# A graph network kernel planned in ticks: which instructions of a tick come first

## The chip, the cores and the metric

The kernel runs on one core of one Trainium2 chip. The metric is the device time of one launch in microseconds (us). The engines of the core are TensorE (PE, with its weight loads as PEld), VectorE (DVE), ScalarE (ACT), GpSimd (POOL) and SyncE (SP, which here only issues transfers). Each runs its own list of instructions in the order in which the kernel gives them, and waits at an instruction until its inputs are there and its output's buffer is free.

## The reference

There are 64 graphs of 256 nodes with 256 features. Two layers follow each other, each with its own residual.

```python
# layer 0: three steps of a gated graph network, one GRU cell for all of them
h = jnp.maximum(_layernorm(x), 0.0)
A = (adj != 0).astype(x.dtype)
for i in range(3):
    m = jnp.einsum('bnd,de->bne', h, weight[i])
    aggr = jnp.einsum('bst,bsd->btd', A, m)
    gi = aggr @ w_ih.T + b_ih          # split in three: i_r, i_z, i_n
    gh = h @ w_hh.T + b_hh             # split in three: h_r, h_z, h_n
    r, z = sigmoid(i_r + h_r), sigmoid(i_z + h_z)
    n = tanh(i_n + r * h_n)
    h = (1.0 - z) * n + z * h
x = x + h
# layer 1: graph attention, four heads of 64
h = jnp.maximum(_layernorm(x), 0.0) @ W.T + b
logits = leaky_relu(l_src[:, :, None, :] + l_dst[:, None, :, :], 0.2)
probs = softmax(where(adj == 1, logits, -9e15), axis=2)
x = x + einsum('bijh,bjhc->bihc', probs, h)
```

## The kernel before

Two graphs make a pair, and there are 32 pairs. What is wide is 512 columns: two graphs (halves 0 and 1) of 256 nodes each. A tile such as `hT` holds the features on the partitions, in two groups of 128 (`c` = 0, 1), and the nodes of both graphs along the columns.

**The GRU step** is the class `Step` (L365), one object for each pair and layer, with its work cut into `tick_0` to `tick_5`. A `block` (L289) is four f32 matmuls of 128 by 256 that add one weight matrix times one half of the columns to a PSUM bank; the profile counts each of them as two instructions. A `part` (L394) is one such matmul. The two graphs share products: instead of weights times half 0 and weights times half 1, the kernel multiplies sums and differences of the halves and of the weights, and puts the results together with VectorE and ScalarE. That is why there are `T1`, `T2`, `T3`, `T4` (sums of state and aggregate, two groups each) and `T2n`, `T3n`, `T4n` (sums of the state for n's term alone). `state_sums` (L381) makes `T1` and the three n sums. In short:

- `tick_0`: the parts `N00` and `NS1` into bank `qa`, ScalarE's copies `qb` and `m5n`, 16 matmuls that sum the neighbours into `pa`, ScalarE's copy to `aggr`, VectorE's `T3` and `T2`.
- `tick_1`: the parts `N01` and `NS2`, VectorE's sum in `qb` (L435), the block `RH` and its copy.
- `tick_2`: the parts `NS3` and `NS4`, VectorE's `hn` (L445), the block `S1`, `T4`.
- `tick_3`: the block `S2`, VectorE's sum into `pe`, the block `RA`, and the tanh that makes gate r for half 0.
- `tick_4`: the part `N11`, ScalarE's `hn`, the block `RZ`, VectorE's sum into `Z`, the block `S4`, and r for half 1.
- `tick_5`: for each half `input_n` (L469), which has VectorE write (r + 1) times hn into the bank `pn` (L472) and then adds the block `NA` to it; between them the block `ZA` for gate z. Then `new_n`: a tanh on ScalarE and a difference on GpSimd (L484).
- `update(0)` and `update(1)`, four VectorE instructions (L498, L499), write the new state over the old.

`back` (L540) transposes the new state for the next step's neighbour sum, or adds it to x after the last one. Then come the second norm, `values`, `score_rows`, `linked`, `barred_in`, `add_rows`, `maxima` (L685, two VectorE instructions for each head), `leaky`, `exps` and `output` for the attention. Score rows and maxima go through DRAM, to be read back on all partitions.

**The plan.** Nothing orders these pieces but one table, `plan`. Each is put at a tick (`at`, L307) and in one of three phases of that tick; the kernel then walks the ticks, and in each tick the phases in the order of their numbers, and in a phase the later pair first. A new pair starts every `APART` = 18 ticks, and a step of six ticks is followed by six that belong to a step of a neighbouring pair. So a repeat of 18 ticks has three steps: layer 0 of a new pair, layer 2 of the pair before it, and layer 1 of the new pair, while an older pair goes through its attention.

```python
READY, STEP, REST = range(3)
...
for tick in sorted(plan):
    for phase in plan[tick]:
        for _, fn in sorted(phase, key=lambda y: y[0]):
            fn()
```

`STEP` holds the six ticks of a GRU step; norms, sums, updates, maxima, leaky and exps are put in `READY`, transposes, values and output in `REST`. Most tiles have one buffer; x has five, adj two. PSUM has five banks for the step (`gate_bank`) and three for everything else (`bank`).

Of the kernel before, what the change touches and what calls it, by code (L numbers as in the profile page):

```python
# [14 lines left out]
ALU = mybir.AluOpType  # L15
AX = mybir.AxisListType

P = 128
# [8 lines left out]
def gated_gnn_then_gat_kernel(  # L27
# [39 lines left out]
    nc = tc.nc  # L67
    B, N, D = x.shape
# [4 lines left out]
    KD = D // P  # L73
# [3 lines left out]
    T = PB * N  # L77
# [31 lines left out]
    out_rows = out.rearrange("b s d -> (b s) d")  # L109


    def load_adj(p, name):
        at = buf("adj", [P, R, N], f"{name}_{p}", I32)
        nc.sync.dma_start(at, adj_rows[ts(p, T), :].rearrange("(r q) t -> q r t", q=P))
        return at

    def load_x(p):
        xt = buf("x", [P, R, D], f"x_{p}")
        nc.sync.dma_start(xt, x_rows[ts(p, T), :].rearrange("(r q) d -> q r d", q=P))
        return xt  # L120
# [69 lines left out]
    w_a = [const.tile([P, KD, 6 * D], F32, name=f"w_a_{l}") for l in range(L)]  # L190
    RH, RZ = range(2)
    N00, N01, N11, NS1, NS2, NS3, NS4 = range(7)
    RA, ZA, NA, S1, S2, S4 = range(6)
# [95 lines left out]
    def block(pt, w, j, src, start=False):  # L289

        for c in range(KD):
            for k in range(KD):
                nc.tensor.matmul(  # L293
                    pt[:, ts(c, N)], w[:, k, j * D + c * P : j * D + (c + 1) * P], src[:, k, :],
                    start=start and c == 0 and k == 0, stop=(c == KD - 1 and k == KD - 1),
                    skip_group_check=True,
                )
# [1 line left out]

    READY, STEP, REST = range(3)
    SUB = 6
    APART = 3 * SUB
    plan = {}
# [1 line left out]
    def at(tick, phase, p, fn):  # L307
        plan.setdefault(tick, ([], [], []))[phase].append((-p, fn))

    def plan_norm(src, name, p, ticks):  # L310

        v = {}

        def stats(r0):
            def fn():
                if not v:
                    v["st"] = small.tile([P, R, 6], F32, tag="st", name=f"st_{name}")
                    v["mv"] = small.tile([P, R, 2], F32, tag="mv", name=f"mv_{name}")
                for r in (r0, r0 + 1):
                    nc.vector.bn_stats(v["st"][:, r, :], src()[:, r, :])  # L320
                    nc.vector.bn_aggr(v["mv"][:, r, :], v["st"][:, r, :])
            return fn

        def deviation():
            rstd = v["rstd"] = small.tile([P, R], F32, tag="rstd", name=f"rstd_{name}")
            nc.vector.tensor_scalar_add(rstd, v["mv"][:, :, 1], EPS)
            nc.gpsimd.tensor_tensor(rstd, rstd, mhalf, ALU.pow)

        def result():
            xn = v["xn"] = buf("xn", [P, R, D], f"xn_{name}")  # L330
            for r in range(R):
                nc.vector.tensor_scalar(  # L332
                    xn[:, r, :], src()[:, r, :], v["mv"][:, r, 0:1], v["rstd"][:, r : r + 1],
                    op0=ALU.subtract, op1=ALU.mult,
                )

        for t, fn in zip(ticks, (stats(0), stats(2), deviation, result)):
            at(t, READY, p, fn)
        return v
# [19 lines left out]
    def by_c(y):  # L359
        return y.rearrange("q (c n) -> q c n", c=KD)  # L360

    def of(y, i):
        return y[:, :, ts(i, N)]

    class Step:  # L365
# [15 lines left out]
        def state_sums(self):  # L381
            h0, h1 = of(self.hT(), 0), of(self.hT(), 1)
            T1 = self.own("T1", [P, KD, N])
            nc.vector.tensor_sub(T1, h1, h0)  # L384
            T3n = self.own("T3n", [P, N])
            nc.vector.tensor_sub(T3n, h1[:, 1, :], h1[:, 0, :])
            T2n = self.own("T2n", [P, N])
            nc.vector.tensor_sub(T2n, h1[:, 1, :], T1[:, 0, :])
            T4n = self.own("T4n", [P, N])
            nc.vector.tensor_sub(T4n, T2n, h0[:, 1, :])  # L390

# [12 lines left out]
        def tick_0(self, hN, edge):  # L406
            h0 = of(self.hT(), 0)
            q_a, q_b = self.bank("qa"), self.bank("qb")
            self.part(q_a[:, :N], N00, h0[:, 0, :], start=True)
            self.part(q_a[:, N:], NS1, self.T1[:, 0, :])  # L410
            nc.scalar.copy(q_b[:, :N], q_a[:, :N])
            nc.scalar.copy(self.own("m5n", [P, N]), q_a[:, N:])
            aggr = self.own("aggr", [P, KD, T])
            for e in range(KD):
                pt = bank(f"pa_{self.n_}_{e}")
                for i in range(PB):
                    for s in range(KN):
                        for half in range(2):
                            nc.tensor.matmul(  # L419
                                pt[:, ts(i, N)], hN[half][:, i * KN + s, ts(e, P)], edge[:, i * KN + s, :],  # L420
                                start=(s == 0 and half == 0), stop=(s == KN - 1 and half == 1),
                            )
                nc.scalar.copy(aggr[:, e, :], pt)  # L423
            T3 = self.own("T3", [P, KD, N])
            nc.vector.tensor_sub(T3, of(aggr, 1), of(self.hT(), 1))  # L425
            nc.vector.tensor_add(self.own("T2", [P, KD, N]), T3, h0)

        def tick_1(self):
            h0 = of(self.hT(), 0)
            q_a, q_b = self.qa, self.qb  # L430
            self.own("hn", [P, KD, T])
            self.part(q_a[:, :N], N01, h0[:, 1, :])
            self.state_n(0, 0, q_a[:, :N])
            self.part(q_b[:, :N], NS2, self.T2n)
            nc.vector.tensor_add(q_b[:, N:], q_b[:, :N], self.m5n)  # L435
            p_c = self.bank("pc")
            block(p_c, w_h, RH, h0, start=True)
            self.bank("p5")
            nc.scalar.copy(self.bank("pd"), p_c)

        def tick_2(self):
            q_b = self.qb
# [17 lines left out]
        def tick_4(self):  # L460
            Z_ = self.own("Z", [P, KD, T])
            self.part(self.qb[:, :N], N11, self.T4n)
            self.state_n(1, 0, self.qb[:, :N])
            block(self.pd, w_h, RZ, self.T3)
            nc.vector.tensor_add(of(Z_, 1), by_c(self.pd), by_c(self.m5))
            block(self.pe, w_a[self.l], S4, of(self.aggr, 1))
            self.tanh_half(1, self.R, by_c(self.pe), 0)

        def input_n(self, i):  # L469

            p_n = self.bank(f"pn{i}")
            nc.vector.scalar_tensor_tensor(  # L472
                by_c(p_n), of(self.R, i), 1.0, of(self.hn, i), op0=ALU.add, op1=ALU.mult
            )
            block(p_n, w_a[self.l], NA, of(self.aggr, i))

        def new_n(self, i):
            n__ = of(self.hn, i)
# [5 lines left out]
            nc.gpsimd.tensor_sub(of(self.R, i), of(self.hT(), i), n__)  # L484

        def tick_5(self):
            self.input_n(0)
            self.tanh_half(1, self.Z, of(self.Z, 1), KD)
            block(self.pd, w_a[self.l], ZA, self.T4)
            self.new_n(0)  # L490
            self.tanh_half(0, self.Z, by_c(self.pd), KD)
            self.input_n(1)
            self.new_n(1)
# [7 lines left out]
    def plan_pair(p):  # L501
        t0 = APART * p
        v = {}

        def ready(t, fn):
            at(t0 + t, READY, p, fn)
# [4 lines left out]
        def rest(t, fn):  # L511
            at(t0 + t, REST, p, fn)


        if p == 0:
            v["x"], v["adj"] = first
        else:
            rest(-14, lambda: v.update(x=load_x(p), adj=load_adj(p, "adj")))

        def to_edge():  # L520
            v["edge"] = buf("edge", [P, R, N], f"edge_{p}", F32R)
            nc.vector.tensor_scalar(v["edge"], v["adj"], 0.0, None, op0=ALU.not_equal)

        xn_a = plan_norm(lambda: v["x"], f"a{p}", p, [t0 - 8, t0 - 7, t0 - 6, t0 - 5])
        ready(-4, to_edge)
        h = plan_relu_T(xn_a, "hT_a", f"a{p}", p, [t0 - 4, t0 - 3])


# [6 lines left out]
            nc.vector.scalar_tensor_tensor(lo, flat(xn_a["xn"]), 0.0, hi, op0=ALU.max, op1=ALU.subtract)  # L535

        ready(-3, first_hi)
        ready(-2, first_lo)

        def back(l, i):  # L540

# [17 lines left out]
        for l in range(L):  # L559
            g = Step(f"{p}_{l}", l, lambda: h["hT"])  # L560
            t = 2 * SUB * l
            ready(t - 1, g.state_sums)
            step(t, lambda g=g: g.tick_0(v["hN"], v["edge"]))
            for k, fn in enumerate((g.tick_1, g.tick_2, g.tick_3, g.tick_4, g.tick_5), 1):
                step(t + k, fn)
            ready(t + SUB, lambda g=g: g.update(0))
            rest(t + SUB, lambda g=g: g.update(1))
            for i in range(PB):
                rest(t + SUB + 1 + i, back(l, i))

# [152 lines left out]
        for u in units:  # L723
            t = 47 if last and u.start == 0 else 51
# [35 lines left out]

        for t, (i, j) in zip((60, 61, 62, 63), ((0, 0), (0, 1), (1, 0), (1, 1))):
            ready(t, exps(i, j))
        for r, t in enumerate((62, 63, 64, 66)):
            rest(t, output(r))
        rest(67, lambda: nc.sync.dma_start(out_rows[ts(p, T), :].rearrange("(r q) d -> q r d", q=P), v["x"]))


    at(SUB, REST, 0, lambda: step_weights(1))
# [38 lines left out]
```

## Time and profile before

| what | value |
|---|---|
| time, median of 2 runs | 3209.2 us (3208.84 to 3209.55) |
| span of the profiled run | 3207.4 us |
| mean granted TensorE clock | 0.932 |
| L472 on VectorE, 128x512, one | 694 ns |
| state sums on VectorE: `T1`, `T3n`, `T2n`, `T4n` | 671, 420, 415, 425 ns |
| L685 on VectorE, one head's maximum | 512 ns |
| new state, L498 and L499, one | 688 and 692 ns |
| tanh on ScalarE, 128x256, one | 471 ns |
| L484 on GpSimd, one | 1279 ns |

The busy share of an engine is an average over the span, and a busy TensorE need not run at its full clock: the page has a row for the granted clock in forty slices.

```profile
PE   6888888888888888888888888888888888888875
DVE  4456655555655555665555565555555555565554
PEclk8999999999999999999999999999999999999995
```

All slices between the first and the last two look alike, so what is true of one repeat of 18 ticks holds for nearly the whole run. A line of groups (line, engine, operation, out<-in, count | busy us, mean ns | idle before us, releaser) tells how long an engine stood still just before these instructions, and which instruction let it go on.

### The profile page before, as it was taken

How to read it: one execution, taken by the hardware profiler on the slowest of the kernel's cores; microseconds unless marked ns; L12 is line 12 of the kernel's file. 1: busy time of each engine (PE TensorE's matmuls, PEld its weight loads, DVE VectorE, ACT ScalarE, POOL GpSimd, SP SyncE). 2: the span in 40 equal slices, each digit the busy share in tenths (PEclk: the TensorE clock that was granted, in tenths of full speed). 3: DMA queues.
4: the chain of work that ended last, by engine and by line, in shares of the span. 5: the costliest groups of instructions: out<-in, count | busy, mean ns of one | idle time of the engine just before them, and what ended most of it. 6: DMA issues, size and time to landing. Idle time of an engine off the chain costs nothing.

```text
span 3207.4 us, 38372 instructions
## 1 busy us (share of the span) xinstructions
PE 2720.1 (85%) x14074; PEld 2366.8 (74%) x14074; DVE 1823.8 (57%) x4497; ACT 1485.2 (46%) x3077; POOL 567.4 (18%) x518
## 2 busy tenths in 40 slices
PE   6888888888888888888888888888888888888875
PEld 4777777777777777777777777777777777777765
DVE  4456655555655555665555565555555555565554
ACT  1345444454444454444454444454444554444543
POOL 0011111111112121212111212111211111211112
PEclk8999999999999999999999999999999999999995
DMA  2013224342223342233332233432233432243334
GB/s 72 9 50 72 57 67 93 86 93 67 58 68 93 86 93 56 61 76 93 86 90 54 59 82 86 93 84 48 67 87 86 93 80 47 66 92 86 80 80 99
DMA packets 120317, 239.87 MB, mean 75 GB/s; under 512 B 9792, under 2 KB 79424, under 8 KB 120128
## 3 DMA queue, kind: packets, MB, share of 16 engines
q0 software_dynamic: 34272, 132.13, 21.4%
q1 hardware_dynamic: 80160, 102.52, 10.5%
q10 hardware_dynamic: 5696, 2.76, 0.3%
q8 instruction: 111, 1.82, 0.2%
q14 instruction: 78, 0.64, 0.1%
HBM read 219.82 MB, written 17.56 MB: 74 GB/s over the span
## 4 chain that ended last, share of the span: by engine, by line
PE 71%; DVE 22%; ACT 3%; issue 2%; DMA 1%; POOL 0%; ACTq 0%; SPq 0%; DVEq 0%; POOLq 0%
PE pd L293 17%; PE pn L293 13%; PE pc L293 7%; PE p L293 6%; PE po L745 6%; PE qb L395 5%; PE pa L419 4%; PE pv L596 4%; PE pe L293 3%; DVE any L685 2%; PE qa L395 2%; DVE pn L472 2%; DVE T L384 2%; PE pback L548 2%; DVE xn_a L332 2%
## 5 line engine op out<-in xcount | busy, mean ns | idle before, releaser
L293 PE MATMUL pn<-aggr,w_a 128*128 128x256 f32 x1536 | 445.9, 441 | 297.9 <-DVE pn L472 297.9
L293 PEld LDWEIGHTS pn<-aggr,w_a 128*128 128x128 f32 x1536 | 326.5, 218 | 378.1 <-DVE pn L472 325.1
L484 POOL TENSOR_TENSOR R<-hT_a,hn 128x512 f32<-128x512 f32 x192 | 245.6, 1279 | 1517.1 <-ACT hn L481 1493.0
L498 DVE SCALAR_TENSOR_TENSOR R<-Z,R 128x512 f32<-128x512 f32 x192 | 132.2, 688 | 503.1 <-ACT Z L402 501.5
L293 PE MATMUL pd<-T,w_a 128*128 128x256 f32 x1536 | 399.5, 407 | 0.0
L481 ACT ACTIVATE hn<-pn,bi 128x256 f32<-128x256 f32 x384 | 161.3, 471 | 493.7 <-PE pn L293 493.7
L293 PEld LDWEIGHTS pd<-T,w_a 128*128 128x128 f32 x1536 | 318.8, 211 | 53.2
L685 DVE CUSTOM_DVE_ANT_0 any<-drow,noedge 128x256 f32<-128x256 f32 x512 | 262.3, 512 | 18.2 <-DMA drow<-score_dram 9.2
L745 PEld LDWEIGHTS po<-val,zz 128*128 128x128 f32 x2048 | 256.7, 201 | 15.1 <-ACT zz L736 11.9
L745 PE MATMUL po<-val,zz 128*128 128x65 f32 x2048 | 256.0, 281 | 11.1 <-ACT zz L736 11.1
L713 ACT ACTIVATE zz<-zz,val 128x256 f32<-128x256 f32 x512 | 230.9, 507 | 7.7 <-DMA zz<-score_dram 7.7
L758 POOL TENSOR_TENSOR x<-x,o 128x256 f32<-128x256 f32 x128 | 101.0, 789 | 671.9 <-DVE o L753 671.9
L293 PE MATMUL p<-T,w_a 128*128 128x256 f32 x768 | 214.2, 430 | 0.0
L398 ACT ACTIVATE hn<-qb,bhn 128x256 f32<-128x256 f32 x192 | 90.8, 473 | 249.6 <-DVE hn L445 208.2
L402 ACT ACTIVATE R<-pc,brz 128x256 f32<-128x256 f32 x192 | 80.6, 471 | 264.6 <-PE pc L293 264.6
L425 DVE TENSOR_TENSOR T<-aggr,hT_a 128x512 f32<-128x512 f32 x96 | 66.5, 693 | 224.4 <-ACT aggr L423 224.4
L293 PEld LDWEIGHTS p<-T,w_a 128*128 128x128 f32 x768 | 167.0, 217 | 28.6
L402 ACT ACTIVATE R<-pe,brz 128x256 f32<-128x256 f32 x192 | 80.6, 471 | 220.4 <-PE pe L293 220.4
L293 PE MATMUL pc<-aggr,w_a 128*128 128x256 f32 x768 | 181.4, 379 | 0.0
L293 PE MATMUL pc<-hT_a,w_h 128*128 128x256 f32 x768 | 181.4, 379 | 0.0
L293 PE MATMUL pd<-T,w_h 128*128 128x256 f32 x768 | 181.4, 379 | 0.0
L293 PE MATMUL pe<-aggr,w_a 128*128 128x256 f32 x768 | 181.4, 379 | 0.0
(147 smaller groups left out, 5381.7 us busy)
## 6 DMA issues: line engine op xcount, KB each, us to landing
zz<-score_dram POOLq DMA_DIRECT2D x64, 1024.0 KB, 12.0
zz<-topT_dram POOLq DMA_DIRECT2D x62, 1024.0 KB, 9.6
adj<-in_adj_dram SPq DMA_DIRECT2D x64, 512.0 KB
drow<-score_dram SPq DMA_DIRECT2D x64, 512.0 KB
x<-in_x_dram SPq DMA_DIRECT2D x32, 512.0 KB
out_dram<-x SPq DMA_DIRECT2D x32, 512.0 KB
score_dram<-score SPq DMA_DIRECT2D x128, 4.0 KB
topT_dram<-topT SPq DMA_DIRECT2D x128, 2.0 KB
```

What stands on the lines that cost most here:

```text
L293: nc.tensor.matmul(pt[:, ts(c, N)], w[:, k, j * D + c * P : j * D + (c + 1) * P], src[:, k, :], start=start and c == 0 and k == 0, stop=(c ...
L395: nc.tensor.matmul(pt, w_n[:, j, :], src, start=start, stop=True, skip_group_check=True)
L402: nc.scalar.activation(of(dst, i)[:, c, :], src[:, c, :], AF.Tanh, bias=brz[:, g0 + c : g0 + c + 1], scale=0.5)
L419: nc.tensor.matmul(pt[:, ts(i, N)], hN[half][:, i * KN + s, ts(e, P)], edge[:, i * KN + s, :], start=(s == 0 and half == 0), stop=(s == KN ...
L481: nc.scalar.activation(n__[:, c, :], p_n[:, c, :], AF.Tanh, bias=bi[:, 2 * KD + c : 2 * KD + c + 1])
L484: nc.gpsimd.tensor_sub(of(self.R, i), of(self.hT(), i), n__)
L498: nc.vector.scalar_tensor_tensor(d_, of(self.Z, i), 1.0, d_, op0=ALU.add, op1=ALU.mult)
L596: nc.tensor.matmul(pt[:, :VW], hb["hT"][:, k, ts(r, P)], w_val[:, k, :], start=(k == 0), stop=(k == KD - 1),)
L685: nc.vector.tensor_tensor_reduce(any_, drow[r // KN][:, h, :], v["noedge"][:, r, :], 1.0, -3.0e38, ALU.add, ALU.max, accum_out=v["top"][:, ...
L713: nc.scalar.activation(zz[:, h, :], zz[:, h, :], AF.Prelu, alpha=ALPHA, bias=v["val"][:, r, S0 + H + h : S0 + H + h + 1],)
L745: nc.tensor.matmul(po[:, ts(h_, VC)], logits[i][:, j, h_, ts(s, P)], v["val"][:, i * KN + j, ts(h_, VC)], start=(j == 0), stop=(j == KN - 1),)
L758: nc.gpsimd.tensor_add(v["x"][:, r, :], v["x"][:, r, :], o)
```

## The change

The phases change places: in each tick the step's own work now comes first. `T3` and `T2` go from the end of tick 0 to the end of tick 1, the part `NS1` and its copy behind the neighbour sum, and the write of (r + 1) times hn is taken out of `input_n` as `first_n`: half 0 goes into tick 4, half 1 to the top of tick 5. The sums of the state are made at tick 3 of the step in between (`t - 3`) for layers 1 and 2, and `T4n` on its own at tick 2. The second update goes from `REST` to `READY`. The first norm, the edges and the loads of x and adj get other ticks, `first_lo` another phase, and the last row of the output comes a tick earlier. The aim is that instructions for which TensorE waits don't stand behind others in the lists of VectorE and ScalarE.

```diff
@@ -299,7 +299,7 @@
-    READY, STEP, REST = range(3)
+    STEP, READY, REST = range(3)
     SUB = 6
     APART = 3 * SUB
     plan = {}
@@ -386,8 +386,9 @@
             nc.vector.tensor_sub(T3n, h1[:, 1, :], h1[:, 0, :])
             T2n = self.own("T2n", [P, N])
             nc.vector.tensor_sub(T2n, h1[:, 1, :], T1[:, 0, :])
-            T4n = self.own("T4n", [P, N])
-            nc.vector.tensor_sub(T4n, T2n, h0[:, 1, :])
+
+        def last_state_sum(self):
+            nc.vector.tensor_sub(self.own("T4n", [P, N]), self.T2n, of(self.hT(), 0)[:, 1, :])
@@ -407,9 +408,7 @@
             h0 = of(self.hT(), 0)
             q_a, q_b = self.bank("qa"), self.bank("qb")
             self.part(q_a[:, :N], N00, h0[:, 0, :], start=True)
-            self.part(q_a[:, N:], NS1, self.T1[:, 0, :])
             nc.scalar.copy(q_b[:, :N], q_a[:, :N])
-            nc.scalar.copy(self.own("m5n", [P, N]), q_a[:, N:])
             aggr = self.own("aggr", [P, KD, T])
             for e in range(KD):
                 pt = bank(f"pa_{self.n_}_{e}")
@@ -421,9 +420,8 @@
                                 start=(s == 0 and half == 0), stop=(s == KN - 1 and half == 1),
                             )
                 nc.scalar.copy(aggr[:, e, :], pt)
-            T3 = self.own("T3", [P, KD, N])
-            nc.vector.tensor_sub(T3, of(aggr, 1), of(self.hT(), 1))
-            nc.vector.tensor_add(self.own("T2", [P, KD, N]), T3, h0)
+            self.part(q_a[:, N:], NS1, self.T1[:, 0, :])
+            nc.scalar.copy(self.own("m5n", [P, N]), q_a[:, N:])
         def tick_1(self):
             h0 = of(self.hT(), 0)
@@ -437,6 +435,9 @@
             block(p_c, w_h, RH, h0, start=True)
             self.bank("p5")
             nc.scalar.copy(self.bank("pd"), p_c)
+            T3 = self.own("T3", [P, KD, N])
+            nc.vector.tensor_sub(T3, of(self.aggr, 1), of(self.hT(), 1))
+            nc.vector.tensor_add(self.own("T2", [P, KD, N]), T3, h0)
         def tick_2(self):
             q_b = self.qb
@@ -461,18 +462,20 @@
             Z_ = self.own("Z", [P, KD, T])
             self.part(self.qb[:, :N], N11, self.T4n)
             self.state_n(1, 0, self.qb[:, :N])
+            self.first_n(0)
             block(self.pd, w_h, RZ, self.T3)
             nc.vector.tensor_add(of(Z_, 1), by_c(self.pd), by_c(self.m5))
             block(self.pe, w_a[self.l], S4, of(self.aggr, 1))
             self.tanh_half(1, self.R, by_c(self.pe), 0)
+        def first_n(self, i):
+
+            nc.vector.scalar_tensor_tensor(
+                by_c(self.bank(f"pn{i}")), of(self.R, i), 1.0, of(self.hn, i), op0=ALU.add, op1=ALU.mult
+            )
+
         def input_n(self, i):
-
-            p_n = self.bank(f"pn{i}")
-            nc.vector.scalar_tensor_tensor(
-                by_c(p_n), of(self.R, i), 1.0, of(self.hn, i), op0=ALU.add, op1=ALU.mult
-            )
-            block(p_n, w_a[self.l], NA, of(self.aggr, i))
+            block(getattr(self, f"pn{i}"), w_a[self.l], NA, of(self.aggr, i))
         def new_n(self, i):
             n__ = of(self.hn, i)
@@ -484,6 +487,7 @@
             nc.gpsimd.tensor_sub(of(self.R, i), of(self.hT(), i), n__)
         def tick_5(self):
+            self.first_n(1)
             self.input_n(0)
             self.tanh_half(1, self.Z, of(self.Z, 1), KD)
             block(self.pd, w_a[self.l], ZA, self.T4)
@@ -515,14 +519,14 @@
         if p == 0:
             v["x"], v["adj"] = first
         else:
-            rest(-14, lambda: v.update(x=load_x(p), adj=load_adj(p, "adj")))
+            rest(-20, lambda: v.update(x=load_x(p), adj=load_adj(p, "adj")))
         def to_edge():
             v["edge"] = buf("edge", [P, R, N], f"edge_{p}", F32R)
             nc.vector.tensor_scalar(v["edge"], v["adj"], 0.0, None, op0=ALU.not_equal)
-        xn_a = plan_norm(lambda: v["x"], f"a{p}", p, [t0 - 8, t0 - 7, t0 - 6, t0 - 5])
-        ready(-4, to_edge)
+        xn_a = plan_norm(lambda: v["x"], f"a{p}", p, [t0 - 14, t0 - 13, t0 - 13, t0 - 7])
+        ready(-1, to_edge)
         h = plan_relu_T(xn_a, "hT_a", f"a{p}", p, [t0 - 4, t0 - 3])
@@ -535,7 +539,7 @@
             nc.vector.scalar_tensor_tensor(lo, flat(xn_a["xn"]), 0.0, hi, op0=ALU.max, op1=ALU.subtract)
         ready(-3, first_hi)
-        ready(-2, first_lo)
+        rest(-3, first_lo)
         def back(l, i):
@@ -559,12 +563,13 @@
         for l in range(L):
             g = Step(f"{p}_{l}", l, lambda: h["hT"])
             t = 2 * SUB * l
-            ready(t - 1, g.state_sums)
+            ready(t - 3 if l else t - 1, g.state_sums)
+            ready(t + 2, g.last_state_sum)
             step(t, lambda g=g: g.tick_0(v["hN"], v["edge"]))
             for k, fn in enumerate((g.tick_1, g.tick_2, g.tick_3, g.tick_4, g.tick_5), 1):
                 step(t + k, fn)
             ready(t + SUB, lambda g=g: g.update(0))
-            rest(t + SUB, lambda g=g: g.update(1))
+            ready(t + SUB, lambda g=g: g.update(1))
             for i in range(PB):
                 rest(t + SUB + 1 + i, back(l, i))
@@ -760,9 +765,9 @@
         for t, (i, j) in zip((60, 61, 62, 63), ((0, 0), (0, 1), (1, 0), (1, 1))):
             ready(t, exps(i, j))
-        for r, t in enumerate((62, 63, 64, 66)):
+        for r, t in enumerate((62, 63, 64, 65)):
             rest(t, output(r))
-        rest(67, lambda: nc.sync.dma_start(out_rows[ts(p, T), :].rearrange("(r q) d -> q r d", q=P), v["x"]))
+        rest(66, lambda: nc.sync.dma_start(out_rows[ts(p, T), :].rearrange("(r q) d -> q r d", q=P), v["x"]))
     at(SUB, REST, 0, lambda: step_weights(1))
```

## What the change is expected to do

> **What bounds the kernel now.** I read the page's engine shares first, then the waits, then one repeat of the work as stretches, and last the timeline and the chain of waits at one gap.
>
> ```profile
> PE 2720.1 (85%) x14074; PEld 2366.8 (74%) x14074; DVE 1823.8 (57%) x4497; ACT 1485.2 (46%) x3077; POOL 567.4 (18%) x518
> ...
> L293 PE MATMUL pn<-aggr,w_a 128*128 128x256 f32 x1536 | 445.9, 441 | 297.9 <-DVE pn L472 297.9
> L293 PE MATMUL pd<-T,w_a 128*128 128x256 f32 x1536 | 399.5, 407 | 0.0
> L293 PE MATMUL pe<-aggr,w_a 128*128 128x256 f32 x768 | 181.4, 379 | 0.0
> ```
> ```profile
> PE pn L293 <- DVE pn L472: 297.9, 95, 5.4
> PE qb L395 <- DVE qb L435: 117.9, 65, 4.7
> PE ptopT L610 <- DVE top L697: 12.4, 3, 6.1
> ```
>
> TensorE is the busiest engine, and it stands still for 487 us of the span. Two waits are 416 us of that, both on VectorE, which is itself busy only 57%: so VectorE is not too slow, it does other things first. The pn matmuls also run longer than the same matmuls elsewhere (mean 441 ns against 379 for pe).
>
> ```profile
> 1512.50:1547.00 34.50, 29.14 (x145) 25.00 (x143) 23.81 (x58) 16.96 (x39) 5.70 (x6) 0.90 0.05 16
> 1547.00:1579.00 32.00, 30.60 (x168) 26.96 (x167) 15.18 (x30) 19.80 (x39) 8.48 (x7) 1.00 0.68 154
> 1579.00:1611.00 32.00, 25.39 (x132) 22.12 (x131) 17.27 (x52) 9.81 (x20) 3.54 (x4) 0.89 0.31 61
> ```
>
> These stretches (length, then busy PE, PEld, DVE, ACT, POOL, then clock, DMA share, GB/s) are about one repeat of 18 ticks. Where PE has few gaps the clock is 1.00; in the two with gaps it is 0.90 and 0.89. One gap in full, from the timeline and the chain:
>
> ```profile
> 1597.47 0.18 DVE L751 RECIPROCAL rden<-po 128x4 f32<-128x4 f32 x1 [2.56 <-PE po L745]
> 1597.76 0.42 DVE L753 TENSOR_TENSOR o<-po,rden 128x256 f32<-128x256 f32 x1
> 1598.10 0.42 DVE L320 BATCH_NORM_STATS2 st_a<-x 128x6 f32<-128x256 f32 x1
> ...
> 1599.18 0.66 DVE L384 TENSOR_TENSOR T<-hT_a 128x512 f32<-128x512 f32 x1
> ...
> 1600.89 0.42 DVE L685 CUSTOM_DVE_ANT_0 any<-drow,noedge 128x256 f32<-128x256 f32 x1
> ```
> ```profile
> 1595.70 1.75 PE po L745 x16
> 1599.27 0.57 DVE T L384
> 1601.78 0.62 DVE pn L472
> 1602.45 3.78 PE pn L293 x8
> 1606.23 2.75 PE pd L293 x8
> 1608.98 1.73 PE pn L293 x8
> ```
>
> PE ends po at 1597.45 and waits 5 us for one VectorE instruction (L472), which stands behind a norm, the state's sums and the maxima, none of which it needs. Then it pays again: eight pn and eight pd matmuls take 6.53 us where two warm blocks take 3.46.
>
> [...] clock 0.89 to 0.90 where gaps of 3.3 and 5.0 us lie, 1.00 where the longest is 1.4 us, and blocks of 3.78 us beside 1.73. [...] so I count PE by starts of warm blocks, from the chain, and not by its 85%.
>
> **PE's own work in a repeat.** Three layer steps make a repeat: slot A (ticks 0 to 5, a new pair's layer 0), B (layer 2 of the pair before), C (layer 1). From the warm rows of the chain: a block 1.73, two parts 0.86, the 16 aggr matmuls 1.92, po 1.73, two value rows 1.81, a transpose group 0.44. A step is 9 x 1.73 + 7 x 0.43 + 1.92 = 20.5. The rest of a pair is 4 po, 2 x 1.81, ten transpose groups and about 1 us of small ones: 16. So 3 x 20.5 + 16 = 77.4 us. The trace has qa of slot A at 202.13 (pair 2) and 2996.69 (pair 31): 29 repeats of 96.4. So 19.0 us in each are waits and half clock (13 of them the two waits, 416 us over 32).
>
> **The change part by part.** No arithmetic comes or goes; each edit moves instructions.
>
> 1. L472 for the first half goes to tick 4, behind its hn only, ahead of the Z sum; the second half to the top of tick 5. The norms', sums' and maxima's work then comes after them. In B: RA ends at 14.0 us from the slot's start, po at 15.8, N11 at 16.2; ScalarE's hn follows at 16.9 (0.47), VectorE's pn0 at 17.65 (0.69). PE needs it after RZ, S4 and po, 21.4: no wait. pn1 comes after rden and o (0.6) of that po, at 22.9; PE needs it at 24.8. In A pn0 is done about 1.9 us early. In C ScalarE has R, hNhi_a, leaky and hT_a ahead of hn (0.84 + 1.07 + 0.91 + 0.60 from RA's end at 12.9), so hn ends at 16.8, pn0 at 17.5, and PE was ready at 17.2: about 0.45 us stays. The gaps of 1.4, 5.0 and 3.3 us become 0, 0, 0.45.
>
> 2. L435, ahead of the next qb matmul, loses T3 and T2 (1.4 us) in front of it and, being first in tick 1, the maxima (0.8) and in C xn_a (1.7, now a tick earlier). Both updates (4 x 0.69) now come before it in tick 0; the second waits for n's tanh and 1.3 us of GpSimd, and is done 3.4 to 3.8 us into the slot. Behind that wait stand maxima and L435. L435 runs at about 4.7 in B and C, 5.1 in A; PE wants its bank at 5.8 (B, C) and 8.4 (A). No wait, with about 1 us to spare. Its other consumer, ScalarE's hn (L398, 118.8 us behind the update), starts earlier too.
>
> 3. Moving three state sums to tick 3 of A and B puts 1.4 us ahead of the score copy in A, which PE's transpose needs: PE waits about 0.8 us there. This is the one new PE wait I find. In B they lie beside po. T4n (0.42) lies beside the S1 block. For layer 0 sums, edge and noedge (2.9) follow pn1 in C, beside ZA and pn1's block.
>
> 4. NS1 after aggr, tanh ahead of leaky and exps, output one tick earlier: order alone. The ScalarE copies for aggr fit: n's tanh ends 1.0 us into a slot, qb's copy at 2.5 in A's wake (a barred write of 1.06 between), and PE needs it at 3.2.
>
> 5. x and adj load at -20. The adj buffer is free only when edge of the pair before has run, now three ticks later; so the load waits on SyncE for that, with the topT rows queued behind it, and GpSimd's add waits for those. That is some 2 us late, against about three ticks (13 us) until the add. adj has a repeat to land.
>
> Sum: 77.4 + 0.8 + 0.45 = 78.7. I allow 1.0 for small waits that I have not seen, as the margins of item 2 are about 1 us: 79.7 against 96.4, 16.7 us a repeat, 29 x 16.7 = 484. Ahead of pair 2 lie some 13 us of such waits, of which I take 11; after 2996.69 some 24 (4.48, 4.71 and 2.71 are the long ones, with half clock behind them), of which I take 15, since loads and ScalarE bound the last pair. 3209 - 484 - 26 = 2699, so 2700.
>
> **Rivals.** Half the gain: the wait moves. For: VectorE will hold 55 us of work (57% of 96.4) in a repeat of 80, [...] and update(1)'s wait on GpSimd now stands ahead of L435; if ScalarE's tanh comes late by 1 to 2 us, L435 and pn1 slip and the clock drops again. At half of the 19 us left: 87.5, so 3209 - 29 x 8.9 - 15 = 2936. Against: VectorE has 25 us idle, and each margin of item 2 was counted with its load in it.
> No change: PE is dense, [...] Against: one core runs here, and 32 us at 30.60 busy kept 1.00.
> Slower: the late adj or topT rows hold VectorE or ScalarE. If a pair stood 20 us more for them, 2700 + 29 x 20 = 3280. Against: the copies have ticks to spare, and the DMA share above is 0.05 to 0.68.
>
> **How the numbers follow.** Forecast 0.73 (2627 with every wait gone, to 2790), half the gain 0.20, no change 0.03, slower 0.04. The time is the forecast's 2700. The range 2630 to 2850 takes in the forecast and the nearer part of the second case. Faster 0.93, same 0.03, slower 0.04.
>
> **What would show it.** Right: PE behind pn under 40 us and behind qb under 20; pn's mean near 379 ns; PE at about 95%, DVE near 67% (1823.8 of 2700); mean clock about 0.98; about 25 us of new waits at pscore. Wrong: waits of pn or qb over 100 us in all (item 1 or 2), a clock below 0.95 without gaps, or waits named DMA on edge, any or zz (item 5).

## The result, and the profile after

The changed kernel takes 2689.4 us (2689.2 to 2689.7, 2 runs), against 3209.2 before: a ratio of 0.838 (95% interval 0.834 to 0.842). Forecast were 2700 us, and 2630 to 2850 as the range. The shares, the row of the granted clock and the group of pn on the page of the changed kernel:

```profile
PE 2564.9 (95%) x14074; PEld 2259.6 (84%) x14074; DVE 1853.6 (69%) x4497; ACT 1466.7 (55%) x3077; POOL 653.4 (24%) x518
...
PEclk9899999999999999999999999999999999999995
...
L293 PE MATMUL pn<-aggr,w_a 128*128 128x256 f32 x1536 | 367.0, 382 | 0.0
```

The counts of each engine's instructions are those of before. TensorE stands still for 123 us of the span instead of 487, and is busy for 155 us less with the same matmuls: 365 + 155 = 520 us, the whole gain. The pn matmuls wait for nothing, and at 382 ns each they run nearly as fast as those of pe (379 ns). The first lines of TensorE's waits after:

```profile
PE qa L396 <- ACT m5n L424: 35.9, 66, 0.6
PE pscore L615 <- DVE score L636: 18.8, 33, 2.0
PE ptopT L615 <- DVE top L702: 13.1, 3, 5.8
```

Neither pn nor qb is in this list any more. What leads it are two new waits, of which the prediction had only the second.

One repeat of slots C, A and B as three stretches (length, busy PE, PEld, DVE, ACT, POOL, clock, DMA share, GB/s):

```profile
1508.95:1532.64 23.69, 23.17 (x125) 20.21 (x125) 20.51 (x53) 14.47 (x33) 5.19 (x4) 1.00 0.18 55
1532.64:1559.48 26.84, 26.33 (x142) 22.98 (x140) 17.05 (x37) 15.73 (x34) 5.84 (x5) 1.00 0.62 149
1559.48:1588.84 29.36, 28.79 (x176) 26.10 (x174) 19.41 (x49) 15.45 (x30) 9.60 (x9) 1.00 0.37 72
```

This repeat takes 79.9 us, at full clock in all three slots. The qa of slot A starts at 181.79 us for pair 2 and at 2491.26 for pair 31, so the mean of 29 repeats is 79.6, where before it was 96.4.

### The profile page after: what moved, and what is told of

It reads as the page before. It is cut to its first block, busy times and chain, and to the rows that moved or that the text cites. A ratio compares the mean times of both kernels' runs of the same rounds, so it can differ in the third digit from the quotient of the medians.

```text
span 2687.4 us, 38787 instructions
## 1 busy us (share of the span) xinstructions
PE 2564.9 (95%) x14074; PEld 2259.6 (84%) x14074; DVE 1853.6 (69%) x4497; ACT 1466.7 (55%) x3077; POOL 653.4 (24%) x518
## 4 chain that ended last, share of the span: by engine, by line
PE 88%; ACT 5%; DVE 4%; issue 1%; DMA 1%; POOL 0%; ACTq 0%; SPq 0%; DVEq 0%; POOLq 0%
PE pd L293 18%; PE pn L293 12%; PE pc L293 10%; PE po L750 9%; PE qb L396 6%; PE p L293 6%; PE pe L293 6%; PE pa L418 5%; PE pv L601 4%; PE qa L396 4%; PE pback L552 3%; ACT aggr L422 2%; ACT zz L662 1%; PE pt_a L351 1%; PE pt_b L351 1%
## 5 line engine op out<-in xcount | busy, mean ns | idle before, releaser
L487 POOL TENSOR_TENSOR R<-hT_a,hn 128x512 f32<-128x512 f32 x192 | 318.3, 1658 | 930.4 <-ACT hn L484 865.9
L293 PE MATMUL pn<-aggr,w_a 128*128 128x256 f32 x1536 | 367.0, 382 | 0.0
L293 PE MATMUL pd<-T,w_a 128*128 128x256 f32 x1536 | 364.6, 380 | 0.0
L293 PEld LDWEIGHTS pn<-aggr,w_a 128*128 128x128 f32 x1536 | 287.1, 190 | 42.9 <-DVE pn L473 6.2
L293 PEld LDWEIGHTS pd<-T,w_a 128*128 128x128 f32 x1536 | 286.8, 190 | 36.9
L690 DVE CUSTOM_DVE_ANT_0 any<-drow,noedge 128x256 f32<-128x256 f32 x512 | 244.7, 478 | 15.2 <-DMA drow<-score_dram 6.2
L502 DVE SCALAR_TENSOR_TENSOR R<-Z,R 128x512 f32<-128x512 f32 x192 | 131.7, 686 | 147.3 <-POOL R L487 142.6
L558 DVE TENSOR_TENSOR hNlo<-pback,hNhi 128x512 fp32r<-128x512 f32 x128 | 88.5, 691 | 183.0 <-ACT hNhi L557 183.0
L503 DVE SCALAR_TENSOR_TENSOR hT_a<-R,hn 128x512 f32<-128x512 f32 x192 | 174.9, 911 | 13.3
L473 DVE SCALAR_TENSOR_TENSOR pn<-R,hn 128x512 f32<-128x512 f32 x192 | 142.8, 744 | 59.8 <-ACT R L403 31.6
L293 PE MATMUL p<-T,w_a 128*128 128x256 f32 x768 | 181.4, 379 | 0.0
```

The lines of the kernel that those rows point to most:

```text
L293: nc.tensor.matmul(pt[:, ts(c, N)], w[:, k, j * D + c * P : j * D + (c + 1) * P], src[:, k, :], start=start and c == 0 and k == 0, stop=(c ...
L473: nc.vector.scalar_tensor_tensor(by_c(self.bank(f"pn{i}")), of(self.R, i), 1.0, of(self.hn, i), op0=ALU.add, op1=ALU.mult)
L502: nc.vector.scalar_tensor_tensor(d_, of(self.Z, i), 1.0, d_, op0=ALU.add, op1=ALU.mult)
L503: nc.vector.scalar_tensor_tensor(of(self.hT(), i), d_, 0.5, of(self.hn, i), op0=ALU.mult, op1=ALU.add)
L690: nc.vector.tensor_tensor_reduce(any_, drow[r // KN][:, h, :], v["noedge"][:, r, :], 1.0, -3.0e38, ALU.add, ALU.max, accum_out=v["top"][:, ...
```

## The experiments

Theory: time is lost only where an instruction that TensorE needs stands behind others on VectorE, and again in the half clock that follows such a gap. Rivals: one part of the change does it all; the slow matmuls after the gap have a cause other than the clock; or the moved norms and loads matter. Each of the first eight kernels and e11 has one timed run; e9, e10 and e12 have four.

| kernel | us | wait of pn, us | wait of qb, us | clock, 1500 to 2000 us |
|---|---|---|---|---|
| before | 3209 | 297.9 | 117.9 | 0.94 |
| e1, before with phases swapped | 2953 | 111.4 | 83.8 | 0.97 |
| e2, before with pn's write split off | 2896 | 70.8 | 117.5 | 0.97 |
| e11, before with both | 2814 | 0 | 83.5 | 0.99 |
| e5, before with matmuls in the gap | 3078 | 93.4 | 119.1 | 1.00 |
| after | 2689 | 0 | 0 | 1.00 |
| e3, after without the split | 2851 | 108.3 | 0 | 0.99 |
| e4, after with the old phases | 2736 | 42.4 | 3.3 | 1.00 |
| e7, after with T3 and T2 early | 2792 | 0 | 80.2 | 1.00 |
| e6, after with NS1 between the aggr banks | 2690 | 0 | 0 | 1.00 |
| e8, after with the old ticks | 2673 | 0 | 0 | 1.00 |

**e1: the phases alone.**

```diff
-    READY, STEP, REST = range(3)
+    STEP, READY, REST = range(3)
```

> The kernel before with one edit: the phases change places, so that a step's own work comes first in its tick. The write of pn stays in tick 5, T3 and T2 at the end of tick 0, every other tick as before. Theory of the order (each instruction for which TensorE waits gains by what no longer stands ahead of it on VectorE): pn now stands ahead of the state's sums and the maxima of tick 5, but still behind tick 4's norm and rden, so its wait shrinks from 9.3 us a repeat to about 2.6 (0 in A, 1.5 in B, 1.1 in C); L435 still stands behind T3, T2 and both updates, so qb waits about 3.3 a repeat; the clock stays full. Repeat 83.3 us, time about 2790 us, pn wait about 80 us and qb about 105. Rival, the swap of phases is the whole change: 2690 us and both waits under 20. Rival, the swap needs the split of pn to do anything: above 3000 us.

2953 us: between the theory and its second rival. The waits on the new order are about as worked out, but a third one came with it, and the clock did not stay full:

```profile
PE pn L293 <- DVE pn L472: 111.4, 64, 2.2
PE qb L395 <- DVE qb L435: 83.8, 63, 1.8
PE pback L548 <- DVE hT_a L499: 40.0, 64, 1.0
```

`pback` waits for the second update, which in the old plan is in the last phase of tick 0 and now stands behind T3, T2 and the first update. The change moves that update to `READY`, and after it the pback wait is 3.4 us. Idle and busy time account for the loss: against the changed kernel 235 us of these three waits, and 78 us of TensorE busy for longer (2643.0 against 2564.9), less 55 for m5n and pscore, which are not there, make 258 of the 264 us. How much of the 78 is the clock can be estimated from the span and the mean granted clock: 2951.2 x (1 - 0.964) is 106 us, 2687.4 x (1 - 0.983) is 46, so some 60.

**e2: the split alone.**

```diff
             self.state_n(1, 0, self.qb[:, :N])
+            self.first_n(0)
...
         def tick_5(self):
+            self.first_n(1)
             self.input_n(0)
```

> The kernel before with one edit: the write of (r + 1) times hn is taken out of input_n, half 0 to tick 4 behind hn, half 1 to the top of tick 5; phases and ticks as before. Theory of the order: the first half is early, but the second still stands behind what tick 5 has in its first phase (sums, maxima, norm), and is late for the first block by about 1.8 us in B and 0.3 in C, since TensorE has the two blocks NA and ZA to do before the second NA; qb's wait stays at 118 us. Repeat about 83, with half clock perhaps 85: 2790 to 2850 us; the wait of pn 40 to 70 us. Rival, the split alone is the whole change: 2690 us. Rival, the split does little, since the other half keeps the queue: above 3000 us, pn wait above 200.

2896 us, 46 above the expected range. The waits are as expected (71, at the edge, and 118 us). TensorE is busy for 69 us longer than in the changed kernel, where I had allowed some 2 us a repeat, 58 in all, for the clock; that explains a part of the 46 us, and the rest stays open.

**e11: both together, nothing else.** The two edits above in one kernel.

> The kernel before with two edits: the phases change places and pn's write is split off, with T3 and T2, NS1, sums and all ticks as before. Alone they gave 256 and 313 us. Theory: pn's wait goes wholly (each alone left 111 and 71 us of it), and with it the half clock, so that only the wait for qb (84 us with the phases swapped) and for pback (40 us) stay: against the changed kernel these 124 us more, but 41 less for m5n's copy and 19 less at pscore, which came with NS1 and the sums: 2689 + 124 - 60 = 2753 us, clock 1.00 in the steady part. Rival, the two gains add: 3209 - 256 - 313 = 2640. Rival, they overlap, and the other edits carry the rest: 2850 or more.

2814 us, 61 more than expected. The pn wait is gone, as the theory had it: each edit alone leaves some, the two together none. So the parts don't add (256 + 313 = 569 alone, 396 together), because both work on the same wait. Qb and pback keep 83.5 and 39.9 us. The clock was not full: 0.99 over 1500 to 2000 us. The rest to the changed kernel, 125 us, belongs to the other edits and to this clock; e7, where T3 and T2 alone are worth 103 us, points to them above all.

**e3: the split undone in the changed kernel.** `first_n(i)` goes back into `input_n(i)`, just ahead of the block `NA`.

> The changed kernel with one edit undone: pn's write is back in input_n, in tick 5 just ahead of its block, all else as changed. Theory of the order: pn then stands behind tick 4's stats, rden and xn_b: a wait of about 1.0 us in A, 1.5 in B and 1.3 in C, 3.6 us a repeat, without loss of clock: about 2690 + 29 x 3.6 = 2795 us, pn wait about 115 us, qb wait near 0. Rival, with the phases swapped the split is not needed: 2690 to 2705 us. Rival, the split carries the gain: above 3000.

2851 us. The wait was worked out at 115 us and measured at 108; the other 54 us of the loss are TensorE busy for longer (2618.7 against 2564.9). I had expected the clock to stay; by span and mean clock as for e1 (0.972 against 0.983) some 34 of the 54 are the clock, and the rest was not traced. Three starts of pn in its timeline, from slots B, C and B:

```profile
1508.14 3.40 PE L293 MATMUL pn<-aggr,w_a 128*128 128x256 f32 x8 [1.41 <-DVE pn L472]
...
1536.39 1.99 PE L293 MATMUL pn<-aggr,w_a 128*128 128x256 f32 x8 [1.39 <-DVE pn L472]
...
1593.91 3.66 PE L293 MATMUL pn<-aggr,w_a 128*128 128x256 f32 x8 [1.41 <-DVE pn L472]
```

The gaps are alike, 1.4 us. In C, behind f32 blocks, the next eight matmuls take 1.99 us; in B, where po's 65-column matmuls run ahead of the gap, they take 3.40 and 3.66. So a gap of 1.4 us can be enough for the half clock, but neither its length nor the light work ahead decides alone. The whole trace of e3 has 28 such gaps of 1.41 us behind po; 19 are followed by slow matmuls and 9 by fast ones (at 1679.64 us again 1.99). And in e1 none of 28 gaps of the same length behind the same po is:

```profile
1560.62 1.99 PE L293 MATMUL pn<-aggr,w_a 128*128 128x256 f32 x8 [1.41 <-DVE pn L472]
```

What decides between them was not shown.

**e4: the old phases in the changed kernel.** The first diff above, reversed.

> The changed kernel with one edit undone: the phases in the old order, all other edits in. Theory of the order: what was moved by hand (split of pn, T3 and T2, sums at tick 3, norms at other ticks) keeps most of the gain; pn's second half stands behind xn_a and the maxima in B and behind edge, sums and noedge in C (about 0.6 us each), hn on ScalarE behind leaky in C (0.9), and leaky and exps stand ahead of qb's copy: some 2.5 us a repeat, 2760 us. Rival, the phases are what matters: above 2950, with pn wait above 150 us. Rival, the phases do nothing once the rest is moved: 2690 within 10.

2736 us, near the theory's 2760 and far from both rivals. With the other edits in, the order of the phases is worth 47 us, and the wait that comes back is that of pn's second half (42 us in 28 times). So no part carries the gain alone: the swap gives 256 us where nothing else is done, and 47 where all else is.

**e5: the clock by itself.**

```diff
+        def warm(self):
+            pt = bank(f"warm_{self.n_}")
+            for j in range((2, 5, 8)[self.l]):
+                nc.tensor.matmul(
+                    pt[:, :N], w_n[:, N00, :], self.aggr[:, 0, :N], start=(j == 0), stop=True, ...
+                )
         def tick_5(self):
+            self.warm()
             self.input_n(0)
```

> The kernel before with matmuls added in the gap ahead of pn, for nothing but to keep TensorE busy: 2, 5 and 8 f32 matmuls of 128x256 (0.43 us each) at the start of tick 5 of layer 0, 1 and 2, into a bank that nobody reads. They wait for nothing that TensorE does not have. The two waits on VectorE stay where they are. Theory of the clock (the pn and pd blocks after the gap are slow because the clock fell in it): the clock stays at full speed, pn's mean falls from 441 to near 382 ns, and about 5 us a repeat come back: 3209 - 29 x 5 = 3064 us, though TensorE has 6.5 us a repeat more to do. Rival, those blocks are slow for another cause (banks, the weight path, a late operand): no gain, 3200 to 3225 us. Rival, what TensorE does is what counts: slower by up to 29 x 6.5 = 190 us.

3078 us: 135 less than the kernel before on the same chip (3212.9), although TensorE has more to do. By form, the groups of pn and of the added matmuls:

```profile
L293 PE MATMUL pn<-aggr,w_a 128*128 128x256 f32 x1536 | 372.3, 385 | 93.4 <-DVE pn L472 93.4
...
L489 PE MATMUL warm<-aggr,w_n 128*128 128x256 f32 x960 | 224.6, 381 | 0.0
```

The pn matmuls go from 441 to 385 ns each, with their operand about as late as before (225 us of filling and 93 of waiting, 318, where the gap was 298). So the slow blocks came from the clock, and keeping it up gives back about 135 us of the kernel before.

**e7: T3 and T2 back at the end of tick 0.** The three lines that make them return to behind `m5n`.

> The changed kernel with one edit undone: T3 and T2 back at the end of tick 0, where they wait for aggr; all else as changed. Theory of the order: VectorE stands at T3 until aggr is copied (3.1 us into the slot), then does T3, T2 (1.4), both updates (2.8) and the maxima, so that L435 ends at about 8.9 us in C and 7.8 in B, where TensorE wants the bank at 6.5: waits of 2.4 and 1.3 us, 0 in A; 3.7 a repeat, 2689 + 29 x 3.7 = 2796 us, qb wait near 110 us. Rival, the updates wait for GpSimd anyway, so T3 and T2 fill time in which VectorE stands: under 2710.

2792 us against 2796 expected, with a qb wait of 80.2 us where near 110 was expected, at full clock; the other 23 us of the loss are TensorE busy for longer (2587.6 against 2564.9), which was not worked out. The move of these two instructions takes the qb wait away; the swap leaves it (e1), and the split does not touch it (e2).

**e8: the old ticks for norms, edges, loads, `first_lo` and the last output row.**

> The changed kernel with the ticks of the first norm, the edges, the loads of x and adj, first_lo and the last output row as before; phases, split and sums as changed. Theory: VectorE has room in every slot, so these moves are worth little once the step's work comes first: xn_a stands behind L435 in C's tick 1, the stats in B's tick 4 run while TensorE does po, the last po goes back to C's tick 0, where it gives aggr's copies time. Time 2675 to 2720 us. Rival, they carry part of the gain (in B the stats ahead of rden make the second pn late): 2750 or more, pn wait above 50 us. Rival, the early loads matter: waits named DMA on x or adj.

2673 us: 17 less than the changed kernel, on another chip than e12's. These moves bring nothing once the rest is done; one of them costs. No wait on a transfer leads in either kernel.

**e10: only the last output row back.**

```diff
-        for r, t in enumerate((62, 63, 64, 65)):
+        for r, t in enumerate((62, 63, 64, 66)):
...
-        rest(66, lambda: nc.sync.dma_start(...))
+        rest(67, lambda: nc.sync.dma_start(...))
```

> The changed kernel with one edit undone: the last output row and its store go back to ticks 66 and 67 (C's tick 0 in place of B's tick 5). It is to tell which of the old ticks made the run with all of them 17 us faster than the changed kernel. Theory: the row's 1.73 us on TensorE then lies between NS1 and N01 in C and hides the wait for m5n there; half of the 35.9 us of that wait go, with half of the delay beside them: 2668 to 2674 us, the wait for m5n near 20 us in 37 times. Rival, the norms or edges did it: 2686 to 2692 us.

2663.5 us, ratio to before 0.830 (0.828 to 0.831), against 2689.3 and 0.837 (0.836 to 0.839) for the changed kernel on the same chip: 26 us. The wait for m5n is 20.8 us in 37 times, so the mechanism is as expected, half of that wait; the gain is 5 to 11 us over what I worked out. By the profile pages, TensorE stands for 17 us less than in e12 and is busy for 11 us less (2554.2 against 2565.3) with the same instructions; where those 11 come from I did not find. That e8, with the other old ticks too, is 9 us slower than e10 may mean that those cost something; one run of e8, on another chip, does not settle it.

> The changed kernel as it is, on the chip of these runs, for a comparison within it: 2689 us within 0.1%.

This was 2689.3 us (2687.7 to 2689.9).

**e6: the new wait for m5n.** The chain of waits of the changed kernel at the start of slot B shows why TensorE waits there:

```profile
1559.68 0.45 ACT hn L484
1560.13 0.28 issue
1560.41 1.06 ACT zz L662
1561.47 0.28 ACT qb L411
1561.74 0.99 ACT aggr L422 x2
1562.74 0.28 ACT m5n L424
1563.07 0.70 PE qa L396 x2
```

N01 writes one half of bank `qa`, and in this program it waits until ScalarE has read the other half into m5n; that copy stands behind n's tanh, a barred write, qb's copy and both aggr copies.

```diff
                 nc.scalar.copy(aggr[:, e, :], pt)
-            self.part(q_a[:, N:], NS1, self.T1[:, 0, :])
-            nc.scalar.copy(self.own("m5n", [P, N]), q_a[:, N:])
+                if e == 0:
+                    self.part(q_a[:, N:], NS1, self.T1[:, 0, :])
+                    nc.scalar.copy(self.own("m5n", [P, N]), q_a[:, N:])
```

> The changed kernel with one edit more: the part NS1 and its copy m5n go between the two aggr banks instead of behind both. The profile after shows a wait that the prediction did not have: the part N01 waits for m5n's copy of the same bank, 35.9 us in 66 times, about 0.7 us of delay in B and in C each. Theory of the bank (N01 needs the copy done, and the copy stands behind both aggr copies on ScalarE): with NS1 earlier, the copy comes 0.6 us earlier on ScalarE and N01 a part later on TensorE, the wait goes, and 1.4 us a repeat with it: 2689 - 40 = 2650 us. Rival, ScalarE is late in B for other causes (n's tanh and a write of 1.06 us ahead of qb's copy): half of it, 2670. Rival, m5n ahead of aggr delays T3 and costs as much: 2690.

2690 us, no gain. The wait only changed its name:

```profile
PE qa L396 <- ACT qb L411: 44.0, 60, 1.5
```

Now NS1 waits for qb's copy of the same bank. In C the wait went; in A, where none had been, and in B it came back one copy earlier on ScalarE. Neither rival had this: the last one names 2690 us, but for a late T3, of which the waits show nothing.

**e9: a version that beats both.** e8, and two edits more:

```diff
-            self.part(q_a[:, :N], N01, h0[:, 1, :])
-            self.state_n(0, 0, q_a[:, :N])
             self.part(q_b[:, :N], NS2, self.T2n)
...
             block(p_c, w_h, RH, h0, start=True)
+            self.part(q_a[:, :N], N01, h0[:, 1, :])
+            self.state_n(0, 0, q_a[:, :N])
...
-            ready(t - 3 if l else t - 1, g.state_sums)
+            ready(t - 2 if l else t - 1, g.state_sums)
```

> A version to beat both: the kernel with the old ticks for norms, edges, loads and the last output row (2672.5 us), and two edits more. In tick 1 the part N01 and its hn go behind the block RH, so that m5n's copy has 1.7 us more; the sums of the state for layers 1 and 2 go from tick 3 to tick 4, so that they no longer stand ahead of the score copy in A. Theory: the wait for m5n in B (0.57 idle, about 0.68 of delay) and the wait at pscore in A (0.51 idle, about 0.67) both go, 1.35 us a repeat: 2672.5 - 29 x 1.35 = 2633 us, near the 2617 that TensorE's own work sets. Rival, as with NS1 between the aggr banks the wait only changes its name (NS2 then waits for qb's copy on ScalarE, L435 comes later and qb waits): 2660 to 2675. Rival, the sums in tick 4 make the second pn late: above 2680, with a wait of pn.

2619.3 us (2618.2 to 2620.2, 4 runs), ratio 0.816 (0.815 to 0.817), on the same chip 70 us under the changed kernel. That is 14 less than worked out. The wait for m5n is gone and that at pscore is down to 2.4 us; the two edits were not run apart, so each is credited with the wait that it aims at. In the steady part TensorE hardly stands:

```profile
1500.00:2000.00 500.00, 499.44 (x2795) 445.56 (x2794) 356.06 (x871) 292.87 (x615) 125.79 (x101) 1.00 0.45 101
```

Here the work moved is TensorE's own: N01 is not needed before tick 4, so it can wait behind a block for a ScalarE that is late. With PE busy for 499 of 500 us at full clock, order has nothing left to give there; the next gain must come from fewer or cheaper matmuls.

## Why the prediction was right

**The sum.** The 29 repeats were forecast to save 484 us and saved 485 (2794.6 to 2309.5 us). Ahead of pair 2 it was 20 us for 11 forecast, behind pair 31's start 15 for 15. The floor of 77.4 us of TensorE's own work stands as well: in e9, where it hardly waits, slot A's qa starts at 178.88 us for pair 2 and at 2429.94 for pair 31, 77.6 a repeat. Two smaller figures of the prediction do not follow from its sums: half of the 19 us left would be 86.9 us a repeat (2919 us), while 87.5 (2936) is half of the forecast gain; and with every wait gone 3209 - 29 x 19.0 - 26 is 2632, not 2627.

**Item 1, pn.** Right, and by both edits: e1 and e2 each leave part of the wait, e11 none. The 0.45 us that I left in C did not show, but not because C was better than worked out: hn ended 17.2 us into the slot and pn's write 17.9, each 0.4 later than forecast. TensorE came to it only at 18.0 instead of 17.2, late from its wait for m5n, so the write ended just in time.

**The clock.** It was right to count the half clock as part of what the waits cost, and e5 puts it at about 135 us. The picture behind the forecast, that gaps of 3.3 us and more cost the clock and those of 1.4 us don't, was too coarse. e3 lost the clock in most gaps of 1.41 us behind light matmuls (19 of 28), and kept it in 1.39 us behind f32 blocks; the kernel before kept it in about a third of its gaps of 3.3 us in C (10 of 29). The prediction did not suffer, since all gaps of that size went. My expectations for e1, e2 and e3 did: they were 163, 46 and 56 us too low. In e3 the larger part of that is the clock; in e1 it is some 60 us, beside the wait of pback that I had not seen.

**Item 2, qb.** Right: no wait is left, and in C, from the timeline, L435's instruction ends 1.4 us ahead of the matmul that needs its bank, for about 1 forecast; TensorE's own lateness is part of that margin, but in e9, without it, no wait of qb leads either. e7 shows that T3 and T2 in front of it bring 80 us back.

**Item 3, pscore.** Forecast 25 us, measured 18.8.

**Item 4, "order alone".** This step failed. I had followed qb's copy to the part that needs it, but not m5n's, which NS1's new place puts behind both aggr copies: 35.9 us of idle in 66 times. And I had counted the last output row as free, while its old place hid half of that wait: e10 puts it at 26 us. The 1.0 us a repeat that I allowed for waits not seen covered this. It was the right size by luck: nothing in it named m5n, whose two waits alone are 1.1 us of idle a repeat, and it came out because pn's 0.45 did not come and pscore took 0.5 for 0.8.

**Item 5, the loads.** Right: no engine waits on x or adj; SyncE's queue does wait for edge, as forecast (605.6 us in 31 times, before 56.8 in 2), and no other engine waits for these loads. `any` waits 6.2 us for its rows in the whole run, before it was 9.2.

**The rivals.** Dense work kept its clock: 1.00 in all three slots of the repeat above, with TensorE busy for 78.29 of 79.89 us. Half the gain did not come: VectorE's margins held at 69% busy.

## What to carry to other kernels

When a TensorE that is nearly full waits for another engine that is not, ask what stands in that engine's list ahead of the one instruction it waits for, and put the instructions that feed TensorE first. Such a gap can be paid twice, since the clock may fall in it: here it did in every gap of 5.0 us ahead of pn in the kernel before (27 of 27), in 19 of 29 of 3.3 us in C, and in e3, with light matmuls ahead, even in 19 of 28 of 1.4 us. When you move an instruction, follow every reader and the next writer of its bank: the wait that stayed came from a copy whose place nobody had asked about, and was removed by moving a matmul that was not urgent rather than the copy.

## What the runs showed of the hardware

**The clock.** The clock record of the kernel before holds two values, 1.0 and 0.5. There are 76 stretches at 0.5, together 440.8 us, 43 of them 3.41 us long and 29 of 6.83 us. The changed kernel has five, together 94.5 us, and none from 87 to 2574 us. In the kernel before, half clock followed none of 32 gaps of 1.4 us ahead of pn, 19 of 29 of 3.3 us in C, and all 27 of 5.0 us; together with e3 and e1 that says that the length counts and that it does not decide alone. What else does was not shown: no run moved a gap and left the rest.

**VectorE and GpSimd.** Some of their instructions take longer where they overlap, which the denser order makes more common: L503 (before L499) went from 692 to 911 ns in the mean, GpSimd's difference from 1279 to 1658. In the changed kernel 94 of the 192 L503 have no GpSimd instruction beside them and take 0.69 us, and the 30 that overlap a difference take 1.67. The difference takes 1.28 us in the 69 times in which VectorE does nothing beside it, 1.69 beside L502 and L503 (30 times) and 2.88 beside the sums of the state and noedge (30 times), but 1.27 beside L756 and L758 (29 times): not every overlap costs. Two lines of the changed kernel's timeline that overlap:

```profile
1533.32 1.70 POOL L487 TENSOR_TENSOR R<-hT_a,hn 128x512 f32<-128x512 f32 x1 [0.18 <-ACT hn L484]
...
1533.91 1.67 DVE L503 SCALAR_TENSOR_TENSOR hT_a<-R,hn 128x512 f32<-128x512 f32 x1
```

VectorE's instruction, 0.69 us with GpSimd idle, begins while GpSimd's runs and ends 0.56 us after it. Why they take longer was not shown: no run took one of the two away. Of TensorE's waits only pback's 3.4 us are put down to L503, so by its waits it paid next to nothing.
